# Image 3's layer 2 closing and layer 3 projections placed elsewhere in a layer 3 pass, with two small moves between VectorE and ScalarE

## The chip, the cores and the metric

The kernel runs on one core of a Trainium2 chip. The core has TensorE (PE) for matrix products, VectorE (DVE), ScalarE (ACT), GpSimd (POOL) and SyncE (SP), and 16 DMA engines that move data between its memories. Each engine works through its own instructions in the order written, and waits on semaphores for the others. The metric is the time of one execution in microseconds (us), measured on the device.

## What is computed

Four images of 64 x 64 positions and 64 channels pass through four layers, all in fp32. Cut to what matters:

```python
# layer 0: attention over the 4096 positions
q, k, v = x @ Wq + bq, x @ Wk + bk, x @ Wv + bv
x = gamma * (softmax(q @ k.T).T @ v) + x
# layer 1: normalise over channels, 1x1 to 256, 3x3 depthwise, gate, scale by
# channel means, 1x1 back; then normalise, 1x1, gate, 1x1 back; both added to x
# layer 2: each image read as xf, 64 rows (h) of 4096 values (w, c)
xf = xf @ softmax(xf.T @ xf).T + xf   # a symmetric 4096 x 4096 score matrix
# layer 3: embedded attention, 32 features
f = softmax((x @ theta) @ (x @ phi).T)
y = (f @ (x @ g)) @ w + w_b
x = x + batchnorm(y over all four images)
```

Each of layers 0, 2 and 3 has a score matrix of 4096 x 4096 per image. Layers 2 and 3 apply the softmax's divisors after the product; in layer 2 the kernel uses the symmetry, computes a part of the blocks and turns them for the mirrored ones.

## The kernel before

**Stages.** One stream of items is written out by hand: layers 0 and 1 for the four images (layer 1 of one image woven into layer 0 of the next and, for image 3, into layer 2 of image 0), layer 2 of images 0 and 1, then in turn layer 3 of image b and layer 2 of image b + 2, and at the end layer 3 of images 2 and 3 one after the other, and the output. The list `items` holds the main work, `due` (filled by `at(i, fn)`) what is issued right after item i, and two lanes, `conv` (setup and layer 1) and `misc` (loading, features, projections), hand out pieces of smaller work by a counter of microseconds that every item advances: a generator's `yield` says how long to hold its next piece. The order on each engine is exactly this order of issue; no scheduler changes it.

**Layer 3** (`layer3`, L1629) has 64 tiles per image: two blocks `nb` of 32 tiles `mc`. A tile n is 4 banks of scores from TensorE (L1646), exponentials by ScalarE into an e tile of 128 x 2048 (L1657), and two tiles later, in `products(n)` (L1683), the product with the values (L1707). The e tiles live in a pool of six buffers, so tile n + 6 takes the buffer of tile n. PSUM's eight banks are handed out in turn, seven for scores and small pieces and one for the product. For the normalisers all 32 e tiles of a block are summed: VectorE adds most of them into `esum` (L1696, L1698); those in `by_dma` are added by transfers with accumulation instead, two halves of 512 KB each from POOL's queue into one tile `st["dma"]` (L1677, L1679), which VectorE adds once, four tiles after the last (L1700). Four tiles after a block's last tile `totals` sums over partitions on TensorE (L1719).

`BY_DMA` has nine tiles, `MORE_BY_DMA` ten:

```python
BY_DMA = (2, 5, 8, 11, 14, 17, 20, 23, 26)
MORE_BY_DMA = (2, 4, 7, 9, 12, 14, 17, 19, 22, 24)
```

The dictionary `between3` maps an item to a function that `scores(n)` calls after the exponentials of tile n, and to how many banks the first exponential takes. `close2` (L1536) ends layer 2 of an image: sums (L1541 to L1555), then four pieces of eight transposes (L1561), a scaling (L1563) and two additions into x (L1568). `open3` (L1579) makes the next image's projections in six pieces: two for theta (L1589, L1593), two for phi (L1600, L1604), two for the values g (L1609, L1611). `keys3` (L1618) copies phi to all four row groups by sixteen transfers on SP (L1624). For images 0 to 2 these run during layer 2 of the next image; for image 3 (`B - 1`) they run during layer 3 of image 2, and are placed at the end of the listing, where `f` is the first item of image 3's layer 3, so that f - 64 is tile 0 of image 2's:

```python
    for i, gen in enumerate(ends):
        between3[f - 58 + 2 * i] = 3 if 0 < i < 5 else 2, lambda gen=gen: next(gen)
    at(f - 39, lambda: keys3(B - 1))
```

So before the change `close2(3)` takes tiles 6 (sums), 8, 10, 12 and 14, `open3(3)` tiles 16, 18, ... 26, and the keys follow tile 25.

**Layer 2** (`layer2`, L1325) goes through score tiles of 128 x 1024: scores (L1391), two exponentials (L1396), VectorE's stream transposes (L1409) for the mirrored half, products (L1453) and turned products (L1479). For image 0 column sums are accumulated by POOL transfers (L1426) out of the same six e buffers. In this stage PSUM gives three slots of two banks to scores and pieces.

**Normalisation** (`norm`, L1160), twice in layer 1: two halves of x are squared by ScalarE (L1165), TensorE sums x and the squares over channels (L1171, sixteen records), then ScalarE and VectorE make the factor (L1176 to L1180), SP spreads it (L1184), VectorE multiplies (L1192). Image 3's first one is issued as layer 2 of image 0 begins.

**Features** (`features2`, L1303): in four pieces x is transposed on TensorE (L1310); the upper and lower 64 partitions are copied out of PSUM (L1313), the first by VectorE, the second by ScalarE, and SP copies each to the other half. Image 0's run in layer 0 of image 3, image 1's in layer 2 of image 0, those of images 2 and 3 in layer 3 of images 0 and 1.

Of the kernel before, what the change touches and what calls it, by code (L numbers as in the profile page):

```python
# [9 lines left out]
AF = mybir.ActivationFunctionType  # L10
# [681 lines left out]
def fast_path(ctx: ExitStack, tc: tile.TileContext, a: dict, out: bass.AP, bad):  # L692
    nc = tc.nc
    B, H, W, C = a["x"].shape
# [66 lines left out]
    act = nc.scalar.activation  # L761
# [230 lines left out]
    def at(i, fn):  # L992
        due.setdefault(i, []).append(fn)
# [163 lines left out]
            items.append((lambda t=t: item(t), 0.0))  # L1157


    def norm(x, y, first, more):  # L1160


        sq = [new_t("sq"), new_t("sq")]
        for i in range(2):
            act(sq[i], x[:, bass.ts(i, 1024)], AF.Square)  # L1165
            yield first - 2.5 if i else 2.5
        ps = new_ps()
        for i, src in enumerate(((x, x), (sq[0], sq[1]))):
            for j in range(4):
                c = 512 * j if i == 0 else 512 * (j % 2)  # L1170
                mm(  # L1171
                    ps[32 * j : 32 * j + 32, bass.ts(i, 512)], jsel, src[j // 2][:, c : c + 512],
                    start=True, stop=True,
                )
        t = new_t()
        act(t[:, 0:512], ps[:, 0:512], AF.Square)  # L1176
        stt(t[:, 0:512], t[:, 0:512], -1.0, ps[:, 512:1024], ALU.mult, ALU.add)
        yield 4.0
        act(t[:, 0:512], t[:, 0:512], AF.Ln, bias=eps1)
        act(t[:, 512:1024], t[:, 0:512], AF.Exp, scale=-0.5)  # L1180
        yield 3.0
        for j in range(4):
            for h in range(2):
                nc.sync.dma_start(  # L1184
                    out=y[64 * h : 64 * h + 64, bass.ts(j, 512)],
                    in_=t[32 * j + 16 * h : 32 * j + 16 * h + 16, 512:1024]
                    .unsqueeze(1).to_broadcast([16, 4, 512]),
                )
        yield 11.0 + more
        for jp in range(2):  # L1190
            cols = bass.ts(jp, 1024)
            nc.vector.tensor_mul(y[:, cols], y[:, cols], x[:, cols])  # L1192
            yield 1.8
# [6 lines left out]
    def layer1(b):  # L1200
        x = X[:, b]
# [8 lines left out]
                    )  # L1210

        y = xn.tile([128, 2048], F32, tag="xn", name="xn")
        yield from norm(x, y, 5.5 if b == B - 1 else 4.5, 3.0 if b == B - 1 else 0.0)
        yg = new_big("yg")
        yw = yg.rearrange("c (s q p h) -> c p q s h", s=2, p=2, h=H)
        ysum = sm.tile([128, 8], F32, tag="ysum", name="ysum")
# [50 lines left out]
        for j in range(4):  # L1267
# [8 lines left out]
            xs = x[:, bass.ts(j, 512)]  # L1276
# [6 lines left out]
        for j in range(4):  # L1283
# [13 lines left out]
            xs = x[:, bass.ts(j, 512)]  # L1297
# [5 lines left out]
    def features2(b):  # L1303
        x = X[:, b]
        im[b].ko = ko = new_big("ko")
        kv = ko[:, 0:N].rearrange("p (a e n) -> p a e n", e=2, n=128)
        for g in range(4):
            ps = piece()
            for i in range(4):
                nc.tensor.transpose(ps[:, bass.ts(i, 128)], x[:, bass.ts(4 * g + i, 128)], ident)  # L1310
            for e, copy in enumerate((nc.vector.tensor_copy, nc.scalar.copy)):
                own, other = slice(64 * e, 64 * e + 64), slice(64 - 64 * e, 128 - 64 * e)
                copy(kv[own, bass.ts(g, 4), e, :], ps[own, :].rearrange("p (a n) -> p a n", n=128))  # L1313
                nc.sync.dma_start(out=kv[other, bass.ts(g, 4), e, :], in_=kv[own, bass.ts(g, 4), e, :])
            yield 3.7
# [258 lines left out]
    BY_DMA = (2, 5, 8, 11, 14, 17, 20, 23, 26)  # L1574
    MORE_BY_DMA = (2, 4, 7, 9, 12, 14, 17, 19, 22, 24)
    small, between3 = {}, {}
# [41 lines left out]
    def keys3(b):  # L1618
        m = im[b]
        m.ph = new_big("ph")  # L1620
        keys = m.ph.rearrange("p (s n) -> p s n", s=2)
        for j in range(4):
            for k in range(4):
                nc.sync.dma_start(  # L1624
                    out=keys[32 * k : 32 * k + 32, :, bass.ts(j, 512)],
                    in_=m.own[32 * j : 32 * j + 32, :, :],
                )

    def layer3(b):  # L1629
        m, first, last = im[b], len(items), b == B - 1  # L1630
        es, st = {}, {}

        def scores(n):
            nb, mc = n // 32, n % 32
            by_dma = MORE_BY_DMA if b == B - 2 and nb == 0 else BY_DMA
            e = es[n] = new_e()
            if n == 0 and (b < 3 or not turn_of["banks"]):
                take_banks(7)
            if last and n == 62:
                take_banks(6)  # L1640
            banks = [new_bank() for _ in range(4)]
            for kp in range(2):
                for c in range(2):
                    for i in range(2):
                        k = 2 * kp + i
                        mm(  # L1646
                            PS[64 * c : 64 * c + 64, bass.ts(banks[k], 512)],
                            m.ph[32 * k : 32 * k + 32, 128 * mc + 64 * c : 128 * mc + 64 * c + 64],
                            m.th[32 * k : 32 * k + 32, bass.ts(nb, 512)], start=True, stop=True,
                        )  # L1650

            def exp(lo, hi):
                while lo < hi:
                    k = lo + 1
                    while k < hi and banks[k] == banks[k - 1] + 1:
                        k += 1
                    act(  # L1657
                        e[:, 512 * lo : 512 * k],
                        PS[:, 512 * banks[lo] : 512 * banks[lo] + 512 * (k - lo)], AF.Exp,
                    )  # L1660
                    lo = k

            cut = between3[first + n][0] if first + n in between3 else 1
            exp(0, cut)
            if mc == 1 and (nb or last):
                held.append(lambda: exp(1, 4))
            else:
                exp(cut, 4)
            if first + n in between3:
                between3[first + n][1]()  # L1670
            if mc in by_dma:
                if mc == by_dma[0]:
                    st["dma"] = xn.tile([128, 2048], F32, tag="xn", name="xn")
                for h in range(2):
                    cols = bass.ts(h, 1024)
                    if mc == by_dma[0]:
                        nc.gpsimd.dma_start(out=st["dma"][:, cols], in_=e[:, cols])  # L1677
                    else:
                        nc.gpsimd.dma_start(out=st["dma"][:, cols], in_=e[:, cols], accum_op=ALU.add)  # L1679
            for fn in small.get(first + n, []):  # L1680
                fn()

        def products(n):  # L1683
            nb, mc = n // 32, n % 32
            by_dma = MORE_BY_DMA if b == B - 2 and nb == 0 else BY_DMA
            e, esum = es[n], m.tg[:, 2048:4096]
            st["y"] = PS[:, 3584:4096]
            if last and n >= 62:
                st["z"] = PS[:, 3072:3584]
                for k in range(4):  # L1690
                    mm(
                        st["z"][32 * k : 32 * k + 32, :], ones[:, 0:32], e[:, bass.ts(k, 512)],
                        start=n == 62, stop=False,
                    )
            elif mc == 1:
                nc.vector.tensor_add(esum, es[n - 1], e)  # L1696
            elif mc and mc not in by_dma:
                nc.vector.tensor_add(esum, esum, e)  # L1698
            if mc == by_dma[-1] + 4:
                nc.vector.tensor_add(esum, esum, st["dma"])  # L1700
            if last and n == 62:
                return
            if last and n == 63:
                sums(st["z"], False)
            for i in (n - 1, n) if last and n == 63 else (n,):
                for k in range(4):
                    mm(  # L1707
                        st["y"][32 * k : 32 * k + 32, :], m.gx[:, i % 32, :], es[i][:, bass.ts(k, 512)],
                        start=mc == 0, stop=i % 32 == 31,
                    )  # L1710
            if mc == 31 and not (last and n == 63):
                st["yz"] = new_t("yz")
                nc.scalar.copy(st["yz"][:, 0:512], st["y"])
                if held:
                    held.pop()()
# [82 lines left out]
        for n in range(64):  # L1798
# [4 lines left out]
            elif n % 32 == 31:  # L1803
                ends = [(5 if n == 63 and b < 2 else 4, lambda n=n: totals(n))]
# [18 lines left out]
    for b in range(B):  # L1823
        misc_to[len(items)] = True
        f = len(items)
# [3 lines left out]
        else:  # L1829
# [5 lines left out]
            f = len(items)  # L1835
# [5 lines left out]
                    between3[f + i] = 2, lambda turns=turns: next(turns)  # L1841
    f = len(items)
    ends = [close2(B - 1)] * 5 + [open3(B - 1)] * 6
    for i, gen in enumerate(ends):
        between3[f - 58 + 2 * i] = 3 if 0 < i < 5 else 2, lambda gen=gen: next(gen)
    at(f - 39, lambda: keys3(B - 1))
    misc_to[f] = True
    layer3(B - 1)

# [213 lines left out]
```

## Time and profile before

| | us |
|---|---|
| median of 3 runs | 2439.52 (2438.45 to 2439.89) |
| the profiled execution, its own time | 2438.81 |
| its span, first to last instruction | 2437.0 |
| layers 0 and 1 | 0 to 1015 |
| layer 2 of image 0 (with the end of image 3's layer 1) | 1015 to 1322 |
| layer 2 of image 1 | 1322 to 1449 |
| layer 3 of image 0 | 1449 to 1585 |
| layer 2 of image 2 | 1585 to 1782 |
| layer 3 of image 1 | 1782 to 1918 |
| layer 2 of image 3 | 1918 to 2115 |
| layer 3 of image 2 | 2115 to 2264 |
| layer 3 of image 3 | 2264 to 2400 |
| normalisation over all images, output | 2400 to 2437 |

The stages are read from where the first score matmuls of each stand in the timeline. TensorE's granted clock is full (0.999 on average). In a stretch of the profile by windows, busy time of each engine stands beside the share in which the DMA engines moved packets. A timeline line gives start, duration, engine, line, operation, what is written and read, how many instructions were merged, and in brackets the idle time before the first and what ended it.

### The profile page before, as it was taken

To read this page: it belongs to the slowest core of one execution; us is meant where nothing else is said; L and a number is where in the kernel's file an instruction comes from. 1 tells how busy PE (TensorE), PEld (TensorE's weight loads), DVE (VectorE), ACT (ScalarE), POOL (GpSimd) and SP (SyncE) were. 2 spreads that over 40 slices of the span, in tenths; PEclk is the share of its full clock that TensorE was granted. 3 is DMA by queue.
4 is the path that set the end of the run, shared out by engine and by line. 5 is a ranking of instruction groups with operands and counts; after the bars stand their busy time and mean duration, and the time that the engine had idled before them with its cause. 6 is when DMAs were issued, how large, how long until landed. Compare 5 with 4: busy or idle time off the path is not lost.

```text
span 2437.0 us, 63657 instructions
## 1 busy us (share of the span) xinstructions
PE 2408.3 (99%) x27509; PEld 914.1 (38%) x27509; DVE 1461.6 (60%) x1787; ACT 1643.0 (67%) x3140; POOL 553.5 (23%) x395
## 2 busy tenths in 40 slices
PE   9999999999999999999999999999999999999998
PEld 3343453336433543343344442144421344421113
DVE  2020278227832774278667668876668766678886
ACT  4656766666666666668655459954479744579996
POOL 2000000000000000030136562256632365622220
PEclk9999999999999999999999999999999999999999
DMA  3000000010000000030540028710076400386665
GB/s 80 1 18 1 19 1 19 18 19 1 19 18 6 14 19 18 20 77 2 113 97 20 20 65 155 156 28 23 16 153 136 96 21 21 76 169 140 136 136 134
DMA packets 68390, 139.03 MB, mean 57 GB/s; under 512 B 13084, under 2 KB 34309, under 8 KB 68101
## 3 DMA queue, kind: packets, MB, share of 16 engines
q0 software_dynamic: 25040, 89.17, 18.3%
q1 hardware_dynamic: 42309, 43.85, 8.0%
q8 instruction: 218, 3.57, 0.6%
q10 hardware_dynamic: 752, 1.85, 0.2%
q14 instruction: 71, 0.58, 0.1%
HBM read 4.80 MB, written 4.19 MB: 4 GB/s over the span
## 4 chain that ended last, share of the span: by engine, by line
PE 90%; DVE 4%; ACT 4%; issue 1%; DMA 0%; SPq 0%; ACTq 0%; DVEq 0%
PE PS L1096 18%; PE PS L1122 18%; PE PS L1391 10%; PE PS L1453 10%; PE PS L1646 9%; PE PS L1707 9%; PE PS L1479 7%; PE PS L1206 2%; ACT e L1657 2%; DVE tg L1698 1%; ACT e L1396 1%; PE PS L1171 1%; PE PS L1270 1%; PE PS L1561 1%; PE PS L1064 1%
## 5 line engine op out<-in xcount | busy, mean ns | idle before, releaser
L1101 ACT ACTIVATE e<-PS 128x1024 f32<-128x1024 f32 x512 | 523.7, 1023 | 337.7 <-PE PS L1096 301.7
L1396 ACT ACTIVATE e<-PS 128x512 f32<-128x512 f32 x632 | 370.9, 595 | 329.7 <-PE PS L1391 310.5
L1096 PE MATMUL PS<-X,q 64*64 64x512 f32 x4096 | 573.6, 590 | 2.6 <-DVE X L979 1.7
L1122 PE MATMUL PS<-e,vq 64*64 64x512 f32 x4096 | 575.8, 592 | 0.0
L1657 ACT ACTIVATE e<-PS 128x512 f32<-128x512 f32 (+2 forms) x588 | 500.1, 920 | 58.3 <-PE PS L1646 37.5
L1698 DVE TENSOR_TENSOR tg<-tg,e 128x2048 f32<-128x2048 f32 x165 | 377.8, 2290 | 51.1 <-ACT e L1657 40.9
L1391 PE MATMUL PS<-ko 64*64 64x512 f32 x2528 | 334.3, 596 | 0.9 <-DVE X L1568 0.5
L1453 PE MATMUL PS<-e,X 64*64 64x512 f32 x2528 | 327.3, 590 | 1.1 <-ACT own L1465 1.1
L1432 POOL TENSOR_TENSOR esum<-esum,e 128x1024 f32<-128x1024 f32 x132 | 314.0, 2379 | 60.2 <-ACT e L1396 52.9
L1241 DVE SCALAR_TENSOR_TENSOR y<-pad,vec,y 128x1024 f32<-128x1024 f32 x240 | 308.9, 1287 | 18.2 <-ACT y L1237 10.9
L1432 POOL TENSOR_TENSOR esum<-e 128x1024 f32<-128x1024 f32 x22 | 52.2, 2371 | 1177.2 <-ACT e L1396 1171.4
L1409 DVE STREAM_TRANSPOSE turned<-e 128x1024 f32<-128x1024 f32 x196 | 240.6, 1238 | 108.5 <-ACT e L1396 108.2
L1646 PE MATMUL PS<-tg,ph 32*64 32x512 f32 x4096 | 294.9, 612 | 1.7 <-ACT e L1657 0.8
L1096 PEld LDWEIGHTS PS<-X,q 64*64 64x64 f32 x4096 | 182.9, 133 | 262.3 <-issue 181.5
L1122 PEld LDWEIGHTS PS<-e,vq 64*64 64x64 f32 x4096 | 183.5, 133 | 253.3 <-issue 156.3
L1707 PE MATMUL PS<-e,tg 128*32 128x512 f32 x2048 | 272.5, 604 | 0.0
L1679 POOL DMA_DIRECT2D xn<-e x130 | 113.3, 898 | 319.5 <-ACT e L1657 225.9
L1109 DVE TENSOR_REDUCE sums<-zs 128x1 f32<-128x4 f32 x128 | 19.7, 154 | 275.0 <-ACT e L1101 274.8
L1453 PEld LDWEIGHTS PS<-e,X 64*64 64x64 f32 x2528 | 97.5, 133 | 174.1 <-issue 154.4
L1391 PEld LDWEIGHTS PS<-ko 64*64 64x64 f32 x2528 | 90.0, 132 | 167.8 <-issue 145.5
L1646 PEld LDWEIGHTS PS<-tg,ph 32*64 32x64 f32 x4096 | 63.3, 129 | 222.7 <-ACT e L1657 190.2
L1396 ACT ACTIVATION_READ_ACCUMULATOR e<-PS 128x1 f32 x632 | 127.2, 201 | 0.0
(219 smaller groups left out, 1681.2 us busy)
## 6 DMA issues: line engine op xcount, KB each, us to landing
xn<-e POOLq DMA_DIRECT2D x146, 512.0 KB, 5.3
esum<-e POOLq DMA_DIRECT2D x20, 512.0 KB, 5.4
xn<-t SPq DMA_DIRECT2D x64, 128.0 KB
ph<-tg SPq DMA_DIRECT2D x64, 128.0 KB
xn<-X SPq DMA_DIRECT2D x224, 32.0 KB
xr<-X SPq DMA_DIRECT2D x176, 32.0 KB
ko<-ko SPq DMA_DIRECT2D x32, 128.0 KB
xr<-in_x_dram SPq DMA_DIRECT2D x13, 256.0 KB
```

What stands on the lines that cost most here:

```text
L1096: mm(ps[64 * c : 64 * c + 64, bass.ts(r, 512)], m.q[rows_, 128 * t + 64 * c : 128 * t + 64 * c + 64], x[rows_, bass.ts(g, 512)], start=Tru ...
L1101: act(es[g // 2][:, bass.ts(g % 2, 1024)], ps, AF.Exp, bias=SHIFT0, accum_out=zs[:, g : g + 1],)
L1122: ins = mm(PS[64 * s : 64 * s + 64, 2048 + 512 * j : 2560 + 512 * j], vq[rows_, :], es[j // 2][rows_, k : k + 512], start=t == 0 and i < 2 ...
L1241: stt(y1, win, wt, y1, ALU.mult, ALU.add)
L1391: mm(ps[64 * c : 64 * c + 64, bass.ts(r, 512)], m.ko[rows_, k : k + 64], m.ko[rows_, bass.ts(h, 512)], start=True, stop=True,)
L1396: act(e[:, bass.ts(r, 512)], ps[:, bass.ts(r, 512)], AF.Exp, bias=SHIFT2, accum_out=slot(g, 2 * u + r),)
L1432: nc.gpsimd.tensor_add(esum, st["e"][mine_t[h][0]] if k == 1 else esum, e)
L1453: mm(st["acc"][r][64 * c : 64 * c + 64, :], xw[rows_, 4 * g + 2 * u + c, :], st["e"][n][rows_, bass.ts(c, 512)], start=n == mine[h][0], st ...
L1646: mm(PS[64 * c : 64 * c + 64, bass.ts(banks[k], 512)], m.ph[32 * k : 32 * k + 32, 128 * mc + 64 * c : 128 * mc + 64 * c + 64], m.th[32 * k ...
L1657: act(e[:, 512 * lo : 512 * k], PS[:, 512 * banks[lo] : 512 * banks[lo] + 512 * (k - lo)], AF.Exp,)
L1698: nc.vector.tensor_add(esum, esum, e)
L1707: mm(st["y"][32 * k : 32 * k + 32, :], m.gx[:, i % 32, :], es[i][:, bass.ts(k, 512)], start=mc == 0, stop=i % 32 == 31,)
```

## The change

1. `norm` has a new argument `shared`, true for image 3's first normalisation alone. There the second square is a VectorE multiplication, issued before ScalarE's first square; ScalarE makes the first only. The generator yields as often as before.
2. `features2`: for images 0 and 1 both copies are ScalarE's.
3. In layer 3 of image 2 (`b == B - 2`) both blocks, not only the first, use `MORE_BY_DMA`: ten tiles by transfers in the second, and the transferred total added at tile 28 of the block instead of 30.
4. `close2(3)` takes tiles 6, 10, 15, 20 and 25; `open3(3)` takes tiles 44, 46, ... 54, which is in the second block; the keys follow tile 51.

Nothing is computed differently, and the count of instructions on TensorE is the same. On SP the order is the same, too, since nothing stands between the two places of the keys; POOL has two more transfers to issue.

```diff
-    def norm(x, y, first, more):
+    def norm(x, y, first, more, shared=False):
...
         sq = [new_t("sq"), new_t("sq")]
         for i in range(2):
-            act(sq[i], x[:, bass.ts(i, 1024)], AF.Square)
+            xs = x[:, bass.ts(i, 1024)]
+            if shared and i == 0:
+                nc.vector.tensor_mul(sq[1], x[:, 1024:2048], x[:, 1024:2048])
+            if not shared or i == 0:
+                act(sq[i], xs, AF.Square)
             yield first - 2.5 if i else 2.5
...
-        yield from norm(x, y, 5.5 if b == B - 1 else 4.5, 3.0 if b == B - 1 else 0.0)
+        yield from norm(x, y, 5.5 if b == B - 1 else 4.5, 3.0 if b == B - 1 else 0.0, b == B - 1)
...
-            for e, copy in enumerate((nc.vector.tensor_copy, nc.scalar.copy)):
+            for e, copy in enumerate((nc.scalar.copy if b < 2 else nc.vector.tensor_copy, nc.scalar.copy)):
...
         def scores(n):
             nb, mc = n // 32, n % 32
-            by_dma = MORE_BY_DMA if b == B - 2 and nb == 0 else BY_DMA
+            by_dma = MORE_BY_DMA if b == B - 2 else BY_DMA
...
         def products(n):
             nb, mc = n // 32, n % 32
-            by_dma = MORE_BY_DMA if b == B - 2 and nb == 0 else BY_DMA
+            by_dma = MORE_BY_DMA if b == B - 2 else BY_DMA
...
     ends = [close2(B - 1)] * 5 + [open3(B - 1)] * 6
-    for i, gen in enumerate(ends):
-        between3[f - 58 + 2 * i] = 3 if 0 < i < 5 else 2, lambda gen=gen: next(gen)
-    at(f - 39, lambda: keys3(B - 1))
+    for i, gen in zip((6, 10, 15, 20, 25, 44, 46, 48, 50, 52, 54), ends):
+        between3[f - 64 + i] = 3 if 6 < i < 44 else 2, lambda gen=gen: next(gen)
+    at(f - 13, lambda: keys3(B - 1))
```

## The prediction

> **What bounds the kernel now.** I read the busy shares first, then the waits of TensorE by stage, then the timelines around the places that the change touches, then the transfers. Line numbers are those of the kernel before.
>
> ```profile
> PE 2408.3 (99%) x27509; PEld 914.1 (38%) x27509; DVE 1461.6 (60%) x1787; ACT 1643.0 (67%) x3140; POOL 553.5 (23%) x395
> ```
>
> TensorE is never long without work, so the change, which removes none of it, can win only where TensorE stands. In the list of its waits these four are what the change addresses (columns: total us, times, longest):
>
> ```profile
> PE PS L1310 <- ACT ko L1313: 1.5, 3, 0.7
> PE PS L1719 <- DVE tg L1698: 1.1, 1, 1.1
> PE PS L1171 <- ACT sq L1165: 1.0, 1, 1.0
> PE PS L1646 <- DVE X L1568: 0.7, 1, 0.7
> ```
>
> These figures are too small, because a matmul's end is modelled. I take the distance from start to start instead and compare it with the undisturbed distance of the same pair of lines. A layer 3 tile (L1646 and L1707) then takes 2.04 us; a closing piece (eight L1561) adds 1.13, a projection (L1589, L1600) 1.1, a values piece (L1609) 2.0.
>
> TensorE at image 3's first normalisation, in layer 2 of image 0:
>
> ```profile
> 1025.30 1.39 PE L1171 MATMUL PS<-X,jsel 128*32 128x512 f32 x8
> 1026.71 1.05 PE L1171 MATMUL PS<-sq,jsel 128*32 128x512 f32 x4
> 1028.81 1.05 PE L1171 MATMUL PS<-sq,jsel 128*32 128x512 f32 x4 [1.04 <-ACT sq L1165]
> 1029.79 1.95 PE L1391 MATMUL PS<-ko 64*64 64x512 f32 x16
> ```
>
> Sixteen L1171 cost 1.84 us elsewhere and 4.49 here: 2.65 us lost, most of it waiting for the second square, which ScalarE makes behind two exponentials.
>
> TensorE at the features of image 1, and ScalarE there:
>
> ```profile
> 1218.60 1.04 PE L1391 MATMUL PS<-ko 64*64 64x512 f32 x8
> 1220.30 0.65 PE L1310 MATMUL PS<-ident,X 128*128 128x128 f32 x4 [0.66 <-ACT ko L1313]
> ...
> 1226.81 4.53 PE L1479 MATMUL PS<-turned,xr 32*64 32x256 f32 x128
> ```
>
> ```profile
> 1219.66 0.58 ACT L1313 COPY ko<-PS 64x512 f32<-64x512 f32 x1 [1.88 <-DVE ko L1313]
> ```
>
> ScalarE's copy stands until VectorE, behind two stream transposes, has made its own, and the exponentials queue behind it. L1391 to L1310 is 0.97 undisturbed; here it is 1.20, 1.70 and 1.69, and L1479 takes 4.46 for 3.64: 2.5 us lost.
>
> TensorE in layer 3 of image 2, first block, and VectorE at that block's end:
>
> ```profile
> 2151.53 1.07 PE L1646 MATMUL PS<-tg,ph 32*64 32x512 f32 x2
> 2153.33 1.11 PE L1646 MATMUL PS<-tg,ph 32*64 32x512 f32 x14 [0.74 <-DVE X L1568]
> ...
> 2200.65 1.57 PE L1646 MATMUL PS<-tg,ph 32*64 32x512 f32 x16
> 2203.34 1.06 PE L1719 MATMUL PS<-tg,ones 128*32 128x512 f32 x8 [1.12 <-DVE tg L1698]
> ```
>
> ```profile
> 2183.53 0.76 DVE L1611 TENSOR_TENSOR tg<-PS,bc_L_conv_g_b 128x256 f32<-128x256 f32 x2 [3.50 <-ACT e L1657]
> 2184.21 9.47 DVE L1698 TENSOR_TENSOR tg<-tg,e 128x2048 f32<-128x2048 f32 x4
> 2193.71 2.29 DVE L1700 TENSOR_TENSOR tg<-tg,xn 128x2048 f32<-128x2048 f32 x1
> 2196.11 7.09 DVE L1698 TENSOR_TENSOR tg<-tg,e 128x2048 f32<-128x2048 f32 x3
> ```
>
> The fourth closing piece costs 1.7 us at 2151.53. At the block's end L1646 to L1719 takes 2.69 for 1.83 in the other first blocks: 0.9 us, because eight sums run without a gap from 2184.21 to 2203.20, 2.37 us each against 2.04 for a tile. A transferred e tile released late costs 0.2 more at 2192.16. In all 2.8 us.
>
> **What the Trainium skill says.** "VectorE: DVE Perf Modes", section "The perf-mode tier table", gives an fp32 tensor_tensor of 2048 elements 2293 ns at its only speed; the trace agrees (L1698, median 2292 ns), so a sum can't be made cheaper, only moved. "DMA: Bandwidth & Descriptors", section "Issuing engines are not separate DMA queues", says that transfers from SP and POOL share the same 16 engines; the trace agrees: an accumulating half tile takes 5.4 us to land in the median, and 7.8 to 9.2 while the sixteen key transfers are out (2171.8 to 2193.5). "Perfetto Trace Analysis", section "Identifying the Most-Contended Engine", holds busy TensorE to be no measure of headroom; hence the distances above.
>
> **The change, part by part.**
>
> *Features by ScalarE (images 0 and 1).* VectorE loses 8 copies of 0.65 to 0.68 us; ScalarE gains 8 of 0.58 and loses the wait for VectorE. Image 0's lie in layer 0, where ScalarE idles 0.54 to 0.66 us before each exponential and TensorE waits for nothing: 0, and if that cover were gone, 4 x 0.58 = 2.3 us of late slots. Image 1's: per piece ScalarE then has two score tiles at 1.15 and two copies, 3.5 us, against 4.1 of TensorE, so the three late pieces and the late L1479 go: up to 2.5. What is late next is transfers: between 1215 and 1245 the DMA share is 0.96 to 1.01, POOL's column sums (L1426) hold the e buffers, and one exponential at 1247.64 starts only 1.2 us after its buffer came free. TensorE 2.4 us earlier would meet that: 0.8 given back. SP's copies of ko to the other half keep their places. I take -1.7 (bounds -2.5 and 0).
>
> *The square by VectorE.* Added: one 128x1024 tensor_tensor, 1.2 us by the row of L1192. VectorE is idle from 1025.57 to 1029.94, where a stream transpose waits for ScalarE, so the square is done by about 1026.9, as the first one is (1026.66), and delays nothing behind it. The second four L1171 then follow the first and L1391 starts near 1027.75 for 1029.79; its second half needs a slot whose exponentials end at 1028.85, so 1.8 us remain. -1.8 (bounds -2.1 and -0.8).
>
> *Layer 3 of image 2, first block.* Close pieces move from tiles 8, 10, 12, 14 to 10, 15, 20, 25; the six projections (4 x 1.1 + 2 x 2.0 = 8.4 us of TensorE) leave. Each piece takes VectorE 1.23 + 1.42, from 2.34 to 4.94 us after its tile's start, and its banks are wanted at 5.2; between pieces lie three sums, 7.1 us, so VectorE is free again 1.6 us before the next: the 1.7 us stall goes. But what is late next is the block's end. Behind the piece at tile 25 stand nine sums (tiles 23, 25, 26, 27, 28, the transferred total, 29, 30, 31), because the last transferred tile is 24: 4.94 + 9 x 2.37 = 26.3 us after tile 25's start. TensorE reaches L1719 after ten tiles and one piece, 21.5, plus 1.83: 23.4. The stall is 3.1 us in place of 0.9. The values pieces that stood there before gave TensorE 4.0 us of own work while VectorE caught up. That is the step I trust most.
>
> *Transfers in that block.* Still ten tiles, but from tile 4 on a period of 2.5 tiles now takes 5.5 us (less projection work), and the chained halves before came every 6.0 to 6.6 us when pressed (2125.9 to 2153.2). By tile 24 they are some 5 to 6 us behind; a buffer is wanted six tiles after its own, which leaves about 3 to 4 us of slack, and most of the late time falls under the 3.1 us. I take 0.5 (bounds 0 and 4).
>
> *Second block: ten transferred tiles and the projections.* The tenth adds two half-tile transfers (512 KB each) on POOL's queue and takes one sum of 2.3 us from VectorE. Walking VectorE from the last values piece (tile 54): piece done at 4.3 us, sums of 52, 53, 55 to 11.4, then 57 to 60, total, 61 to 63, eight at 2.37: 30.4, against TensorE's 30.5 at the second L1719. Just covered: 0 (up to 1). Banks of the pieces come free 2 us or more before they are wanted.
>
> *Keys.* keys3 moves from tile 25 to 51: sixteen SP transfers that took 21.7 us beside other transfers; nothing else stands on SP between the two places. Phi is written about 38 us after the first L1719 and image 3's scores start at 69, so the keys are there; three transferred tiles (51, 54, 56) now share their time where one and a half did. The last buffer is wanted 13 us after its tile: 0.6, less the 0.2 that goes in the first block: +0.4 (bounds -0.2 and +3).
>
> Sum for layer 3: +3.1 + 0.5 + 0.4 - 2.8 = +1.2. Total: -1.7 - 1.8 + 1.2 = -2.3 us. The profiled execution took 2438.81 (span 2437.0 and 1.8 around it), so 2436.5; the median of the runs, 2439.52, lies 0.7 above it: **2437.2 us**.
>
> **Rivals.**
>
> *All three stalls go (0.25).* VectorE catches up at the end of the first block, and the transfers keep pace: -1.7 - 1.8 - 2.8 = -6.3, 2433.2. For it: VectorE is 60% busy and has lighter load in the first block. Against: the nine sums in a row, each longer than a tile.
>
> *Transfers hold the e buffers (0.12), ending slower than before.* From the point where a transferred tile comes free later than six tiles after it was made, ScalarE waits and with it TensorE. With 6 to 7 us behind in the first block (4 beyond slack), and three tiles at 9 us a half beside the keys in the second (another 4), layer 3 loses 3.1 + 4 + 4 - 2.8 = +8.3, in total +4.8: 2444.3. For it: DMA shares of 0.92 to 1.03 from 2160 to 2192, and buffers released 0.02 us before their use in the second block. Against: TensorE did not stand there.
>
> *The early gains are lost to the full DMA engines (0.10).* Features give 0, the square 0.8, layer 3 +1.2: +0.4, 2439.9.
>
> **How the numbers follow.** The first reading keeps 0.53. A measurement of this kernel tells about 0.2%, 4.9 us, from no change. Faster than 2434.6: the first rival and little of mine, 0.28. Slower than 2444.4: half of the second rival, 0.06. Within: 0.66. The range leaves out the faster end of the first rival and the slower part of the second: 2432.4 to 2442.5; my own case alone would be 2435 to 2440.
>
> **What would show it.** Right: no wait of L1310 for ko, sixteen L1171 in some 2.3 us, no wait of L1646 for X L1568, but L1719 waiting some 3 us for tg L1698 in image 2's first block. Wrong: that last wait under 1.5 us (then the first rival), ScalarE waiting several times for DMA xn in layer 3 (the second), or a wait for DMA esum near 1245 (the third).

## The result and the profile after

The changed kernel takes 2446.36 us in the median (2445.35 to 2450.34, 8 runs) against 2439.06 (2438.45 to 2439.89, 8 runs) before: 1.0032 times the time, 95% interval 1.0022 to 1.0041. It is slower by 7.3 us, where 2.3 us of gain were forecast. The profiled execution took 2446.07 (span 2444.3). Lines from L1165 on stand four further down than before.

The busy shares hide it again:

```profile
PE 2411.6 (99%) x27509; PEld 915.2 (37%) x27509; DVE 1455.6 (60%) x1779; ACT 1646.7 (67%) x3147; POOL 555.3 (23%) x397
```

The early parts did what they should. Timeline of TensorE at image 3's first normalisation:

```profile
1025.60 1.39 PE L1175 MATMUL PS<-X,jsel 128*32 128x512 f32 x8
1027.08 1.07 PE L1175 MATMUL PS<-sq,jsel 128*32 128x512 f32 x8
1028.08 1.97 PE L1395 MATMUL PS<-ko 64*64 64x512 f32 x13
```

Sixteen L1175 now take 2.48 us to the next scores, for 4.49. The waits of L1310 for ko and of L1646 for X are gone from the list of waits as well. The first block of image 2's layer 3 ended with the stall that was forecast, though a shorter one. Timelines of TensorE and VectorE there:

```profile
2190.59 1.57 PE L1650 MATMUL PS<-tg,ph 32*64 32x512 f32 x16
2194.29 1.06 PE L1723 MATMUL PS<-tg,ones 128*32 128x512 f32 x8 [2.13 <-ACT e L1661]
```

```profile
2172.41 11.87 DVE L1702 TENSOR_TENSOR tg<-tg,e 128x2048 f32<-128x2048 f32 x5
2184.31 2.29 DVE L1704 TENSOR_TENSOR tg<-tg,xn 128x2048 f32<-128x2048 f32 x1
2187.06 7.08 DVE L1702 TENSOR_TENSOR tg<-tg,e 128x2048 f32<-128x2048 f32 x3 [0.46 <-DVE tg L1704]
```

Nine sums stand in a row (the five of the first line, the transferred total, three more), and L1723 starts 0.15 us after the last ends at 2194.14. The bracket names ScalarE, but it is VectorE that came last: of several things waited for, read which ended nearest the start.

The loss is in the second block. Timelines of TensorE and ScalarE there, and the list of waits for the whole kernel (total us, times, longest):

```profile
2256.88 1.09 PE L1650 MATMUL PS<-tg,ph 32*64 32x512 f32 x10
2258.71 1.08 PE L1650 MATMUL PS<-tg,ph 32*64 32x512 f32 x6 [0.74 <-ACT e L1661]
...
2262.76 1.09 PE L1650 MATMUL PS<-tg,ph 32*64 32x512 f32 x10
2267.31 1.10 PE L1650 MATMUL PS<-tg,ph 32*64 32x512 f32 x6 [3.46 <-ACT e L1661]
2268.34 1.94 PE L1711 MATMUL PS<-e,tg 128*32 128x512 f32 x8
2270.21 1.80 PE L1650 MATMUL PS<-tg,ph 32*64 32x512 f32 x16
```

```profile
2258.06 3.84 ACT L1661 ACTIVATE e<-PS 128x512 f32<-128x512 f32 x5 [2.13 <-PE PS L1650]
2266.66 3.84 ACT L1661 ACTIVATE e<-PS 128x512 f32<-128x512 f32 x5 [4.76 <-DMA xn<-e]
```

```profile
ACT e L1661 <- DMA xn<-e: 6.7, 3, 4.8
```

TensorE breaks off in the middle of its scores since no bank comes free; ScalarE holds the banks since its next e buffer is still being read by an accumulating transfer, which lands at 2266.56. The shorter break before it ended in the same way, though its bracket names PE: the last half of tile 54 landed at 2257.96, and the exponential that takes its buffer starts at 2258.06. Of the three waits in the list two lie in the first block, 0.98 us each. The kernel before had one, of 0.5 us, late in its first block. Start to start against undisturbed tiles, these lines lose 1.80, 4.54, 0.87 and 0.68 us, 7.9 together; the last two are products and scores that simply run slower (last section).

Two distances carry the whole comparison and are used for every run below. **F** goes from image 1's last L1723 (1927.38 before) to the first of image 2: layer 2 of image 3 and the first block. **S** goes from there to the second L1723 of image 2. Six projections, 8.4 us of TensorE's own work, moved from F to S. F went from 275.96 to 268.44, that is +0.9 after the 8.4; S from 68.35 to 84.64, +7.9 after the 8.4. Everything ahead of F came out 1.5 us shorter, everything behind S is equal: -1.5 + 0.9 + 7.9 = +7.3. The four lines above are all of S's loss.

### The profile page after: what moved, and what is told of

It is laid out like the page before. It is cut to its first block, busy times and chain, and to the rows that moved or that the text cites. A ratio compares the mean times of both kernels' runs of the same rounds, so it can differ in the third digit from the quotient of the medians.

```text
span 2444.3 us, 63677 instructions
## 1 busy us (share of the span) xinstructions
PE 2411.6 (99%) x27509; PEld 915.2 (37%) x27509; DVE 1455.6 (60%) x1779; ACT 1646.7 (67%) x3147; POOL 555.3 (23%) x397
## 4 chain that ended last, share of the span: by engine, by line
PE 90%; ACT 4%; DVE 3%; issue 1%; DMA 1%; SPq 0%; ACTq 0%; DVEq 0%; POOLq 0%
PE PS L1096 18%; PE PS L1122 18%; PE PS L1395 10%; PE PS L1457 10%; PE PS L1650 9%; PE PS L1711 9%; PE PS L1483 7%; ACT e L1661 2%; PE PS L1210 2%; DMA xn<-e 1%; PE PS L1175 1%; PE PS L1274 1%; PE PS L1064 1%; PE PS L1613 1%; PE PS L1299 1%
## 5 line engine op out<-in xcount | busy, mean ns | idle before, releaser
L1457 PE MATMUL PS<-e,X 64*64 64x512 f32 x2528 | 332.0, 590 | 2.0 <-ACT own L1469 1.1
L1683 POOL DMA_DIRECT2D xn<-e x132 | 115.0, 894 | 324.3 <-ACT e L1661 217.5
L1457 PEld LDWEIGHTS PS<-e,X 64*64 64x64 f32 x2528 | 99.0, 133 | 175.8 <-issue 156.2
```

What stands on the lines that cost most here:

```text
L1457: mm(st["acc"][r][64 * c : 64 * c + 64, :], xw[rows_, 4 * g + 2 * u + c, :], st["e"][n][rows_, bass.ts(c, 512)], start=n == mine[h][0], st ...
```

## The experiments

Each kernel was timed in rounds beside the kernel before, whose median lay between 2438.81 and 2439.41 us in them. F and S are read from each one's trace, that is from one execution, which can lie off the median: e2's took 2450.29 us, e5's 2448.35. "Undisturbed" is F 273.2 and S 68.35 with the projections in the first block, F 264.8 and S 76.75 with them in the second (8.4 moved over). The 273.2 is the 275.96 before less the 2.8 us of stalls that the prediction read there. Line numbers of e5 and e6 stand three further down behind the added lines, those of e12 one.

| kernel | median us | ratio to before (95%) | F | S |
|---|---|---|---|---|
| before | 2439.06 | | 275.96 | 68.35 |
| the change | 2446.36 | 1.0032 (1.0022 to 1.0041) | 268.44 | 84.64 |
| e1_early | 2436.03 | 0.9987 (0.9981 to 0.9994) | 275.52 | 68.39 |
| e2_layer3 | 2447.48 | 1.0036 (1.0022 to 1.0050) | 268.33 | 86.71 |
| e3_keys_late | 2445.82 | 1.0027 (1.0018 to 1.0037) | 268.52 | 84.25 |
| e4_nine | 2442.22 | 1.0011 (1.0004 to 1.0017) | 268.55 | 82.72 |
| e5_hold | 2446.08 | 1.0028 (1.0018 to 1.0037) | 268.45 | 87.78 |
| e6_hold_spread | 2439.33 | 1.0002 (0.9994 to 1.0011) | 266.31 | 81.28 |
| e7_closing | 2436.94 | 0.9991 (0.9984 to 0.9997) | 275.41 | 69.68 |
| e8_closing_spread | 2433.72 | 0.9978 (0.9968 to 0.9987) | 273.17 | 68.35 |
| e9_gate | 2438.70 | 0.9998 (0.9990 to 1.0007) | 268.53 | 79.50 |
| e10_gate_nine | 2443.17 | 1.0016 (1.0010 to 1.0023) | 268.55 | 81.93 |
| e11_gate_spread | 2438.06 | 0.9995 (0.9987 to 1.0004) | 266.26 | 80.57 |
| e12_gate_first | 2434.98 | 0.9984 (0.9977 to 0.9992) | 266.25 | 76.75 |

Diffs are against the changed kernel.

**The two halves alone.** e1 keeps the moves between engines and puts back layer 3 of the kernel before; e2 does the reverse.

```diff
 # e1: as before
-            by_dma = MORE_BY_DMA if b == B - 2 else BY_DMA
+            by_dma = MORE_BY_DMA if b == B - 2 and nb == 0 else BY_DMA
... (the same in products)
-    for i, gen in zip((6, 10, 15, 20, 25, 44, 46, 48, 50, 52, 54), ends):
-        between3[f - 64 + i] = 3 if 6 < i < 44 else 2, lambda gen=gen: next(gen)
-    at(f - 13, lambda: keys3(B - 1))
+    for i, gen in enumerate(ends):
+        between3[f - 58 + 2 * i] = 3 if 0 < i < 5 else 2, lambda gen=gen: next(gen)
+    at(f - 39, lambda: keys3(B - 1))
 # e2: as before
-        yield from norm(x, y, 5.5 if b == B - 1 else 4.5, 3.0 if b == B - 1 else 0.0, b == B - 1)
+        yield from norm(x, y, 5.5 if b == B - 1 else 4.5, 3.0 if b == B - 1 else 0.0)
...
-            for e, copy in enumerate((nc.scalar.copy if b < 2 else nc.vector.tensor_copy, nc.scalar.copy)):
+            for e, copy in enumerate((nc.vector.tensor_copy, nc.scalar.copy)):
```

> Only the two moves between engines (second square by VectorE, features of images 0 and 1 by ScalarE); layer 3 as in the kernel before. Theory K (the whole loss comes from the keys and the transferred tiles in the second block): this half of the change gains the 2.1 us by which layer 3 of image 0 began earlier in the changed kernel's trace, so 2437.0 us, ratio 0.9991. Rival E (the two moves were priced rightly at 3.5 us and the layer 3 part costs more than its trace shows): 2435.6. Rival N (the 2.1 us are chance of one execution and the moves give nothing): 2439.1.

> Only the layer 3 part (closing, projections, keys, ten tiles by transfers in both blocks); square and features as in the kernel before. Theory K: layer 3 of image 2 took 8.2 us longer in the changed kernel and all else went 2.1 us better, so this comes out slower than the whole change, near 2448 us (ratio 1.0037). Rival: the two early moves are themselves part of the loss, and this lies at or below the whole change's 2446.4.

Measured: 3.4 us faster and 8.1 us slower (their ratios against the before of their own rounds, 2439.41). So the early moves gain, nearer to rival E's figure than to theory K's and more than the changed kernel's own trace shows, and the whole loss is layer 3's. e2 lies 1.1 us above the whole change, too near for the two intervals to tell.

**The keys issued later, and one transferred tile less.**

```diff
 # e3
-    at(f - 13, lambda: keys3(B - 1))
+    at(f - 6, lambda: keys3(B - 1))
 # e4
-            by_dma = MORE_BY_DMA if b == B - 2 else BY_DMA
+            by_dma = MORE_BY_DMA if b == B - 2 and nb == 0 else BY_DMA
... (the same in products)
```

> The whole change, but the sixteen key transfers follow tile 58 of image 2's layer 3, behind the last transferred tile (56), instead of tile 51. Theory K: the loss of the second block (8.1 us over its undisturbed tiles) is what the keys do to the halves beside them, and all but 1 to 2 us of it goes: 2439 to 2440.5 us. Rival T (ten tiles of halves are too many by themselves, with the projections' tiles or without the keys): the waits for the buffers stay, 2444 to 2446. Rival L (the keys now come too late for image 3's first scores): the second block is whole, but image 3 begins with a wait of 3 us or more for them, 2442 and up, with a wait of L1650 for ph.

> The whole change, but the second block of image 2 has nine tiles by transfers as before (the last three 52, 55, 58 for 51, 54, 56), the keys still after tile 51. Theory K: three halves-pairs still meet the keys, one transferred tile less in some 50 us of the block lets the queue be a little less behind; loses 3 to 6 us of the 8.1 still: 2441 to 2444. Rival T: ten tiles were one too many; with nine the waits for buffers go and VectorE, with one sum of 2.3 us more, becomes late by at most 2: 2438.5 to 2440.5.

e3 seems to refute the keys: S is 84.25 still. But the edit did not do what it says. VectorE's last piece of phi in the timeline of the change, then SP's transfers in the change and in e3:

```profile
2231.73 0.75 DVE L1608 TENSOR_SCALAR tg<-PS,vec 128x512 f32<-128x512 f32 x1 [2.23 <-ACT e L1661]
```

```profile
2232.51 27.97 SPq L1628 DMA_DIRECT2D ph<-tg  x16
```

```profile
2233.38 28.49 SPq L1628 DMA_DIRECT2D ph<-tg  x16
```

They start when VectorE has made phi, wherever they are issued. The kernel lists only TensorE, ScalarE, VectorE and POOL as engines whose written order is kept (`tc.manual_schedule(engines={... PE ... Activation ... DVE ... Pool})`, L2016); SP is not among them, and e5 below shows its order changed. What was said ahead of the prediction of each engine's order holds for those four alone. e3 is thus a repeat of the change and tells nothing on the keys. e4 takes 4.1 us less than the change, as theory K had it, but 6.0 us of loss stay in its S: a tile less helps and doesn't settle it.

One part of S has to be set aside from here on. In e3, e4, e5, e7 and e10 TensorE runs at half its clock for a while behind the first block, which adds 1.3 to 1.6 us to S, and 2.75 in e9 (last section); it has nothing to do with the keys. Without it the loss in S is 7.9 us in the change, 10.0 in e2, 6.1 in e3, 9.7 in e5, which have the same work in the second block but for e5's 32 bytes, and 4.6 in e4. So the loss beside the keys varies by some 4 us between executions.

**A first try to hold the keys, with and without spread tiles.** In both, SP gets a 32-byte transfer out of tile 57's e ahead of the keys; e6 also spreads the ten tiles.

```diff
 # e5 and e6, in scores(n)
+            if b == B - 2 and n == 57:
+                gate = sm.tile([128, 8], F32, tag="ysum", name="gate")
+                nc.sync.dma_start(out=gate[0:1, :], in_=e[0:1, 0:8])
...
-    at(f - 13, lambda: keys3(B - 1))
+    at(f - 6, lambda: keys3(B - 1))
 # e6
-    MORE_BY_DMA = (2, 4, 7, 9, 12, 14, 17, 19, 22, 24)
+    MORE_BY_DMA = (2, 4, 7, 10, 12, 15, 18, 20, 23, 26)
```

> The run before this one moved the issue of the keys without moving their transfers (they began at 2233.4, when VectorE had made phi, since nothing else stands on SP). Here SP's queue is held by one transfer of 32 bytes out of tile 57's e, so that the sixteen keys begin behind the last transferred tile. Theory K (the keys' share of the DMA engines is what makes the halves land late in the second block): halves at 5 to 6 us each, the second block loses under 1.5 us of its 8.1, total 2439 to 2440.5 us. Rival T (ten tiles with accumulation fill the engines by themselves): half or more of the waits stay, 2443 to 2446. Rival L (the keys end too late): image 3 begins late by 2 us or more with waits for ph, 2441 to 2444.

> As the kernel with held keys, and the ten transferred tiles of both blocks spread out to tile 26 in place of 24 (2, 4, 7, 10, 12, 15, 18, 20, 23, 26). Theory tail (the first block's 3.6 us come from the sums that stand in a row on VectorE behind the last transferred tile): two sums fewer stand there, 4.7 us less for VectorE, so that loss falls by 2 to 3 us, and total 2 to 3 us under the held keys. Rival (the row of sums is set by VectorE's whole load in the block, and the later total waits for the last half): within 0.7 us of the held keys, or slower.

Both failed in the same way. SP's timeline in e5:

```profile
2233.04 28.80 SPq L1628 DMA_DIRECT2D ph<-tg  x16
2261.94 1.40 SPq L1686 DMA_DIRECT2D gate<-e  x1
```

The gate, written first, went last. Read by its total alone, e5 would have confirmed rival T. e6, whose keys began at 2228.78, lies 6.8 us under e5, more than its theory asked: in the traces 2.1 in F, as the theory of the tail has it, and 6.5 in S, of which 1.3 is the half clock that e5 has and e6 has not. That tiles further apart leave the queue less far behind when the keys come would explain the rest; no run tests it alone.

**The closing pieces further apart, in e1's kernel.** e8 also spreads the first block's ten tiles.

```diff
 # e7 and e8, on top of e1
-    for i, gen in enumerate(ends):
-        between3[f - 58 + 2 * i] = 3 if 0 < i < 5 else 2, lambda gen=gen: next(gen)
+    for i, gen in zip((6, 8, 11, 14, 16, 18, 20, 22, 24, 26, 28), ends):
+        between3[f - 64 + i] = 3 if 6 < i < 18 else 2, lambda gen=gen: next(gen)
 # e8
-    MORE_BY_DMA = (2, 4, 7, 9, 12, 14, 17, 19, 22, 24)
+    MORE_BY_DMA = (2, 4, 7, 10, 12, 15, 18, 20, 23, 26)
```

> Only the two moves between engines, layer 3 as in the kernel before but with the closing pieces a little further apart: sums at tile 6, pieces at 8, 11, 14, 16, projections at 18 to 28, keys after phi. Theory: the stall of 1.7 us at the fourth closing piece goes and the block's end loses no more than before, 0.5 to 1 us: 2434.3 to 2435.0 us, about 1.4 under the early moves alone (2436.0). Rival: what is taken from that stall comes back at the block's end, as in the change, 2435.7 to 2437.

> As the one with the closing pieces further apart, and the first block's ten transferred tiles spread to tile 26 (its second block keeps nine). Theory tail: both stalls of layer 3 of image 2's first block are gone, 2433.5 to 2434.3 us. Rival: the later transfers meet the keys, which begin near tile 25, and the buffers come free late: 2436 to 2439.

e7 missed its theory by some 2 us. The 1.7 us stall at the fourth closing piece went and came back at the block's end, where TensorE's timeline now has a longer wait:

```profile
2195.07 1.57 PE L1650 MATMUL PS<-tg,ph 32*64 32x512 f32 x16
2199.26 1.93 PE L1723 MATMUL PS<-tg,ones 128*32 128x512 f32 x8 [2.62 <-DVE tg L1702]
```

That is the rival's case: a stall of VectorE's making is moved, not removed, while its work in the block stays. The 1.3 us more in S are the half clock behind that wait. e8 shows what removes the stall: its ten tiles spread, the last at 26. TensorE at the block's end, and SP's keys, in e8:

```profile
2198.78 1.06 PE L1723 MATMUL PS<-tg,ones 128*32 128x512 f32 x8 [0.35 <-ACT e L1661]
```

```profile
2172.29 20.00 SPq L1628 DMA_DIRECT2D ph<-tg  x16
```

F comes out at the undisturbed 273.2, S too, and the kernel, at 2433.72 us, is faster than the kernel before and the changed one. The rival, that the later transfers would meet the keys, was right about the meeting and wrong about its cost: the last three halves took 7.7 to 9.4 us beside the keys, and ScalarE waited for none.

**The keys held in earnest.** What sets the keys' start is phi, so a copy of one column of phi onto itself is put on VectorE, whose order is kept, behind tile 57.

```diff
-    at(f - 13, lambda: keys3(B - 1))
+    def gate():
+        own = im[B - 1].own
+        nc.vector.tensor_copy(own[:, :, 0:1], own[:, :, 0:1])
+
+    at(f - 7, gate)
+    at(f - 7, lambda: keys3(B - 1))
 # e10 besides: nine tiles in the second block, as e4; e11 besides: both blocks spread, as e6
```

> In the two runs before that were to move the keys their transfers still began at 2233, since the place of issue does not set SP's order. Here they can't: a copy of one column of phi onto itself, put on VectorE behind tile 57, is what they wait for. All else as in the changed kernel. Theory K (keys beside the halves make these late): the keys run from about tile 58 on, the halves of 2232 to 2258 take 5 to 6 us for 8 to 9, the second block (first to second L1723, undisturbed 68.35 + 8.4 for the projections = 76.8 us) takes 77 to 78.5 for 84.6 to 87.8, and the total is 2438.5 to 2440.5 us. Rival T (ten tiles alone overfill the queue): 82 us or more, total 2444 and up. Rival L (keys too late): block 77 to 78, then image 3's first tiles wait for ph by 2 us or more, total 2441 to 2443.

> The keys behind tile 57 as in the run beside it, and nine transferred tiles in the second block. Theory K: no different from ten within 1 us (VectorE has one sum more, the engines one tile less): 2438.5 to 2440.5. Rival T: clearly under the ten, by 3 us or more.

> The keys behind tile 57, and the ten transferred tiles of both blocks spread to tile 26. Theory K and theory tail together: the second block at 77 to 78.5 us, the first block 2 to 3 us shorter than in the changed kernel: 2436 to 2438 us. Rival: with tile 58 transferred, the keys meet its halves and the late total waits at the end: 2438.5 to 2441.

e9 settles the main question. SP's timeline, then two stretches by windows (busy us of each engine, then TensorE's clock, DMA share and GB/s), of e9:

```profile
2252.79 14.16 SPq L1628 DMA_DIRECT2D ph<-tg  x16
```

```profile
2235.00:2245.00 10.00, 9.96 (x108) 4.89 (x104) 3.81 (x5) 7.69 (x9) 2.50 (x3) 1.00 0.94 179
2245.00:2255.00 10.00, 10.00 (x121) 1.80 (x113) 9.56 (x7) 7.78 (x9) 2.72 (x4) 1.00 0.90 168
```

The same two stretches of the change:

```profile
2235.00:2245.00 10.00, 9.96 (x112) 4.89 (x104) 4.13 (x6) 6.53 (x8) 1.74 (x2) 1.00 1.03 190
2245.00:2255.00 10.00, 10.00 (x128) 1.88 (x120) 9.37 (x5) 8.83 (x11) 2.61 (x3) 1.00 1.03 194
```

And the halves of L1683 issued from 2231 to 2259, time from issue to landing, in the change and in e9:

```profile
DMA to landing us min/median/max: 4.8/8.2/9.5
```

```profile
DMA to landing us min/median/max: 4.6/5.2/8.1
```

The engines move 190 and 194 GB/s in these two stretches of the change, at a busy share of 1.03. That is the rate of this mixture and not of the engines: two halves that only copy, without accumulation, move at 381 GB/s (last section, at 2192). In the change a part of that is the keys, and a half takes 8.2 us; without them 5.2, no exponential of the second block waits for a transfer, and the total falls by 7.7 us to 2438.70 with the ten tiles untouched. S, at 79.50, is a little above what theory K gave, by the half clock alone: 76.75 and 2.75. Rival T falls, and so does rival L: image 3 begins without a wait for ph.

e10 missed theory K's figure by 2.7 us, e11 its total by little and its S by 2, and they show its condition. There tiles 55 and 58 are transferred, so VectorE has one sum less ahead of the copy and reaches it earlier (keys from 2250.15 and 2245.65), and the keys met the last two tiles; ScalarE waits 2.9 and 3.2 us once, for the last half of tile 58. In e9 the keys began just behind the issue of the last half (2252.12); that one took 8.1 us and nothing waited for it. But meeting the last tiles isn't dear everywhere: in e8 it cost nothing. There two values pieces of 2.0 us each, at tiles 26 and 28, stand between the last transferred tile and the next use of its buffer, and none do in e10 and e11. That this is the difference is likely, and no run tests it alone.

**Both causes undone.** e12 is e9 with the first block's ten tiles, alone, spread to 26.

```diff
 # on top of e9
+    SPREAD = (2, 4, 7, 10, 12, 15, 18, 20, 23, 26)
-            by_dma = MORE_BY_DMA if b == B - 2 else BY_DMA
+            by_dma = (SPREAD if nb == 0 else MORE_BY_DMA) if b == B - 2 else BY_DMA
```

> The keys held behind tile 57 by the copy, the second block's ten tiles as in the change (last at 24), and the first block's ten alone spread to 26. Both causes are then undone, each by itself: theory K keeps the second block free of waits for buffers (no wait of ScalarE for DMA xn there), theory tail takes the stall before the first L1723 (2.5 us over its 1.8) below 1 us, and what trails behind it (some 1.7 us in the run with the keys held alone). Total 2 to 4 us under that run's 2438.7: 2434.7 to 2436.7 us, faster than before, still above the 2433.7 of the kernel that leaves the projections in the first block. Rival: the later sums in the first block come back at the second block's begin or as a late total: 2437.5 to 2439.

2434.98 us, 3.7 under e9. VectorE at the first block's end in e9 and in e12:

```profile
2182.73 2.29 DVE L1704 TENSOR_TENSOR tg<-tg,xn 128x2048 f32<-128x2048 f32 x1
2185.47 7.08 DVE L1702 TENSOR_TENSOR tg<-tg,e 128x2048 f32<-128x2048 f32 x3 [0.46 <-ACT e L1661]
```

```profile
2187.15 2.29 DVE L1705 TENSOR_TENSOR tg<-tg,xn 128x2048 f32<-128x2048 f32 x1
2189.55 2.29 DVE L1703 TENSOR_TENSOR tg<-tg,e 128x2048 f32<-128x2048 f32 x1
```

The row has eight sums in place of nine. The transferred total moves back by two tiles, one sum stands behind it in place of three, and VectorE ends at 2191.84; e9's ended at 2192.55, in an execution that had reached the stage 1.57 us earlier. The wait before L1723 falls from 2.73 to 0.89 us, F by 2.3 us. S is 76.75, just 68.35 + 8.4, so ten transferred tiles and six projections in the second block cost nothing by themselves.

## Why the prediction was wrong

**The square** was priced at 1.8 us. From layer 2's first scores to the first features 1.58 us go in the changed kernel and 1.57 to 1.60 in the eleven others that have the edit. Right within 0.2.

**The features**, 1.7 us with 0 and 2.5 as bounds: from the first features to image 0's layer 3 the twelve executions with the edit are 0.0 to 2.2 us shorter, 1.3 in the mean, 0.55 in the changed kernel's. Up to the first L1483 behind the features all twelve gain the 2.5 us of the forecast, and what is missing in the end is given back within the next 20 us. In the changed kernel it isn't for the reason that the prediction named: no exponential waits for a column sum there, but TensorE stands without a wait (last section). In e1, e4, e7, e8, e11 and e12 an exponential does wait for one, 0.3 to 1.9 us. Together the two were to give 3.5 us; e1, in the median of its runs, gives 3.4.

**The first block**: +3.1 for the row of sums, +0.5 for transfers and -2.8 for stalls that go make +0.8; F shows +0.9. That the sum fits is in part luck, since the terms are shared otherwise: the stall at the end is 1.87 us over the undisturbed distance (2.47 in e9) for 3.1, and about 1.8 us were lost inside the block, where ScalarE waited 0.98 us twice for a transfer, for 0.5. (The prediction's own 26.3 less 23.4 give 2.9, not 3.1.) The row of sums is the cause of the stall at the end, as e8 and e12 show.

**VectorE in the second block**, 0: right, by e12.

**The keys and the transfers of the second block** are the step that failed. The prediction set this out: three transferred tiles share the keys' time, "the last buffer is wanted 13 us after its tile: 0.6", for a term of +0.4 with a bound of +3. Measured: 7.9. The mechanism was there, the term was mis-sized, in two ways. It looked at one late tile and its slack; but the halves accumulate into one tile and are chained: each is issued when the half before it in the same columns has landed, so each one's lateness goes on to the next. From the issue of the first to the landing of the last, eight halves, those of the last four transferred tiles, took 35.8 us in the change (2230.77 to 2266.56) and 28.3 in e9 (2231.92 to 2260.26), and most of these 7.5 us arrive at ScalarE and TensorE: the last half landed 12.7 us after tile 56 was handed to the queue, and ScalarE stood 4.76 us for it. The bytes alone would have warned of it: sixteen transfers of 128 KB are 2.1 MB, an estimated 11 us at the 190 GB/s of these stretches, in a queue with little slack.

Before the change the keys ran beside transferred tiles as well, but later in their block: they followed phi's last piece at tile 22 and met four halves, from 2171.78 on, of which the last three took 7.8 to 9.3 us. The last landed at 2191.62, when its buffer was only just wanted, and 0.2 us were lost. In the change phi's last piece is at tile 50, which is tile 18 of its block, and eight halves met the keys.

And the waits cost more than their length: 1.55 of the 7.9 us are TensorE's lower clock after them (0.56 and 0.58 in the stretches from 2268 to 2272), which the sum did not have.

The second rival described this outcome with 4.8 us, at odds of 0.12. It had the place, and its sign came: ScalarE waited three times for a transfer. Of its two stalls of 4 us the one in the first block came with about 1.8, and the one beside the keys was twice the size.

## What to carry to other kernels

Where chained or accumulating transfers run close to what the engines move, price a transfer put beside them by its bytes over that rate, and take the whole of it as a delay of the chain, less the slack of the chain and not of its last buffer (here an estimated 11 us, of which 7.5 were seen). Such a load belongs behind the chain's last transfers, or where the chain has slack; and here, on a queue whose order is not written out, the producer and not the place of issue decided when it starts, so look at the start in the trace before a run is taken for evidence. The stall that came from VectorE's whole load in the block only wandered when its pieces were moved; spreading the transferred tiles, the last nearer to the block's end, took it away.

## What had not been expected of the hardware

**A wait slows what follows it.** TensorE's timeline in e9 behind the first block, and the same time by windows (the number after POOL's count is the granted clock):

```profile
2192.70 1.94 PE L1723 MATMUL PS<-tg,ones 128*32 128x512 f32 x8 [2.73 <-DVE tg L1702]
2194.38 1.96 PE L1711 MATMUL PS<-e,tg 128*32 128x512 f32 x8
2196.27 2.01 PE L1650 MATMUL PS<-tg,ph 32*64 32x512 f32 x16
2198.21 1.22 PE L1711 MATMUL PS<-e,tg 128*32 128x512 f32 x8
```

```profile
2190.00:2192.00 2.00, 0.00 (x0) 0.00 (x0) 1.90 (x2) 2.00 (x3) 1.11 (x2) 0.94 0.21 84
2192.00:2194.00 2.00, 1.30 (x8) 0.46 (x12) 0.56 (x1) 0.01 (x1) 0.00 (x0) 0.50 0.97 381
2194.00:2196.00 2.00, 2.00 (x12) 0.22 (x4) 1.24 (x2) 0.00 (x0) 0.00 (x0) 0.50 0.15 59
2196.00:2198.00 2.00, 2.00 (x20) 0.33 (x16) 1.90 (x2) 0.00 (x0) 0.00 (x0) 0.50 0.04 8
2198.00:2200.00 2.00, 2.00 (x32) 0.43 (x24) 2.00 (x1) 1.69 (x2) 0.00 (x0) 0.85 0.00 0
```

After 2.73 us without a product the clock is 0.50, products take 1.96 us for 1.07, and S grows by 2.75 us (79.50 for 76.75). In the change the wait of 2.13 us at the same place left the clock at 1.00, while the 3.46 us in the second block halved it. Waits of 2.62 to 2.74 us halved it in e3, e4, e5, e7 and e10 too. The Trainium skill describes such a gate ("TensorE: Matmul & The Clock Gate", section "Part 1: The HAM clock gate"): half rate after an idle window of about 3.4 us that runs freely. The half rate agrees, and so does the length of the window: the 0.94 and 0.85 of the edge stretches put the half rate at 2191.76 to 2198.6, 6.8 us or two such windows. But a shorter idle time than the window was enough: the last scores before the wait end, as modelled, at 2189.97 (2188.40 and 1.57), so the clock fell when TensorE had stood for some 1.8 us. Why 2.62 us are enough and 2.13 are not, no run shows.

**A stand without a wait.** In the changed kernel TensorE stood for 1.48 us from 1230.56 on in the middle of eight products L1457, with nothing that the profile names; e5_hold has 0.86 us at the same place, e1 none. It is most of what the features lost there. Its cause stays open.
